# A graph network in one program: bfloat16 matmuls of the preparation that take the tile size of their neighbours in TensorE's order

## The chip, the cores and the metric

The kernel runs on one NeuronCore of a Trainium2 chip. The metric is the device time of one execution in microseconds. The engines are TensorE (PE in the profile; PEld is its loading of weights), VectorE (DVE), ScalarE (ACT), GpSimd (POOL), and SyncE (SP), which issues most DMAs.

## What is computed

128 graphs of 128 nodes with 64 features go through two layers, each with a residual sum and a layer norm over the features:

```python
mask = (adj > 0.0)
diff = x[:, :, None, :] - x[:, None, :, :]
h = relu((x @ W1a)[:, :, None, :] + diff @ W1b + b1)      # 192 wide
x = layernorm(x + einsum('bjkh,bjk->bjh', h, mask) @ W2 + deg * b2)

agg = adj @ x
h = elu(elu(agg @ V1 + c1) @ V2 + c2)                     # 128 wide
x = layernorm(x + h @ V3 + c3)
```

The adjacency is symmetric in its pattern, about 6% dense, and its entries are drawn at random. The first layer is the costly one: for each node j and each of its neighbours k it needs relu(a_j + c_k), where a and c are projections of x.

## The kernel before

Graphs are taken two at a time: 64 pairs, called rounds here. Within a pair, nodes are sorted by their number of neighbours, so that nodes of like degree stand together in nine blocks (`BLOCKS`, line 43). A block has a range of nodes and a number of slots, one for each possible neighbour; its columns are nodes times slots: 162, 66, 168, 112, 168, 154, 169, 154 and 170 for blocks 0 to 8. A neighbour's c_k is fetched into its column by a matmul with a one-hot matrix.

The steps of a pair, with the lines of the kernel before:

- `prepare` (line 523): the mask and the degrees (DVE, L532), keys (POOL), `spread`, which lays the degrees along the rows by matmul (PE, L545 and L547), ranks by comparison (DVE, L554), the permutation matrix `permb` (DVE, L561).
- `sort_x` (with `project_a`): the features sorted (PE, L578), project_a (PE, L592), the copy `aj` (ACT, L599), then a correction for empty slots: two short matmuls (PE, L612 and L615), the product `ea` (DVE, L621), POOL work.
- `sort_mask` (line 631): mask and permutation sorted and transposed (PE, L637 and L640), copied out (ACT, L645 and L647), the prefix sum along neighbours (PE, L651: one matmul of 256 columns), copied (ACT, L654), and nine writes of one-hot blocks into the tile `oh` (DVE, L661). `oh` is one tile of 128 partitions by 2 x 1323 columns: 1323 for the first graph, then 1323 for the second, each with blocks 0 to 8 in order.
- `turn`: transposes of adjacency and features (PE, L676 and L677). `project_c`: c with 64-row tiles (PE, L694), with a bias (PE, L697), split into three bfloat16 parts `cp`.
- `unit` (line 831), nine times: ACT copies a_j into a PSUM bank (L839), the gather adds c (PE, L851: 18 matmuls in two column tiles of 64, one a graph), DVE sums |.| over slots (L860). Four PSUM banks go round.
- `finish` (line 766): hm (POOL), project (PE, L776, L780, L783), unsort (PE, L793), norm, aggregate (PE, L800), hidden1 (PE, L809), hidden2 (PE, L815), last (PE, L820, L822), norm, output.

TensorE's array is used in three tile sizes: full (128 by 128), two column tiles of 64 (the gathers, the sorting of x, the short correction, aggregate), and two row tiles of 64 (L694). Which is used follows from the operands' shapes.

The order of all work is made in Python while the program is built: `Flow` runs each step as a generator that yields its engine, an assumed cost, the events that it needs and the number of PSUM banks. At each turn `run` takes the step that is ready first by these assumed times, and among those ready within `NEAR` of it (`NEAR_PE` on TensorE) the one with the lowest rank: its due time from the table `DUE`, plus `HOLD` where TensorE would change its mode. Steps in column tiles are marked `PE:t`; all others, row tiles too, count as full. Engines then execute in exactly the order that came out. Waits are added from the tiles that are written and read.

Of the kernel before, what the change touches and what calls it, by code (L numbers as in the profile page):

```python
# [87 lines left out]
class Flow:  # L88
# [6 lines left out]

    LAG = 0.2
    NEAR = 0.1
    NEAR_PE = 0.03  # L100
    SWITCH = 0.1
    HOLD = 0

    def __init__(self, banks):
        self.clock = {}
# [48 lines left out]
    def run(self):  # L154
        while self.threads:
            ready = [(t, th) for t, th in ((self._ready(th[4]), th) for th in self.threads)
                     if t is not None]
            t, th = min(ready, key=lambda r: (r[0], r[1][0], r[1][1]))
            first = th[4][0].split()[0].partition(":")[0]
            near = t + (self.NEAR_PE if first == "PE" else self.NEAR)  # L160
            t, th = min((r for r in ready if r[1][4][0].split()[0].partition(":")[0] == first
                         and r[0] <= near), key=lambda r: self._rank(r[1]))
            engine, cost, after, banks, fn = th[4]
            args = []
            if banks:
                self.free.sort(key=lambda f: f[0])
                args = [self.free.pop(0)[1] for _ in range(banks)]
            fn(*args)
            for e in engine.split():
                e, _, mode = e.partition(":")  # L170
                self.clock[e] = t + cost
                if e == "PE":
                    self.mode = mode
            self._next(th, ([t + cost + self.LAG], *args))


def sparse(tc, env):
# [9 lines left out]
    flow = Flow([ps_m.tile([P, 512], F32, name=f"m{i}") for i in range(4)])  # L187
# [1 line left out]
    EV = {}  # L189


    ROUND = 11.14
    AHEAD = 3
    PACE = ROUND / NB

    DUE = {
        "prepare": (-34.32, -34.43, -29.25, -33.33, -26.26),
        "sort_x": (-25.05, -19.47, -20.79, -15.63, -11.78, -14.33, -11.15, -5.27, -5.97),
        "sort_mask": (-24.98, -24.21, -19.11, -17.63, -31.08, -14.67, -12.13, -9.2, -7.19, -6.42,
                      -4.21, -1.99, -12.24, -7.24),  # L200
        "turn": (-25.52, -21.42),
        "project_c": (-19.53, -25.02, -26.5, -19.03, -18.18, -16.73, -23.86),
        "finish": (7.83, 15.84, 19.72, 16.78, 21.09, 22.6, 28.99, 31.57, 29.07, 31.37, 30.6,
                   34.42, 35.7, 33.91, 37.94, 41.34, 41.72, 43.55, 44, 37.02, 51.36),
        "unit": (-1.1, 0.98, 2.36),
    }

    def pace(u):
# [7 lines left out]
    def event(*key):  # L216
        return EV.setdefault(key, [])
# [13 lines left out]

    def pool(n):
        return 0.15 + n * 0.0022

    def flat(t):
        return t.rearrange("p s n -> p (s n)")
# [22 lines left out]
    iotb = const([P, P], BF16, "iotb")  # L259
# [38 lines left out]
    def made(*names):  # L298
        return [event("const", name) for name in names]
# [223 lines left out]
    def prepare(p):  # L523

        a = ADJ[p]
        d = S[p] = {}
        mk = d["mk"] = prep.tile([P, 2, N], BF16, name="mk")
        deg = prep.tile([P, 2], F32, name="deg")

        def count():  # L530
            for s in range(2):
                nc.vector.tensor_scalar(mk[:, s, :], a[:, s, :], 0.0, 0.0, op0=OP.is_gt,  # L532
                                        op1=OP.add, accum_out=deg[:, s:s + 1])
        ev, = yield ("DVE", 0.54, [event("load", p)], 0, count)
# [6 lines left out]
        ev, = yield ("POOL PORT", 0.43, [ev] + made("jcol"), 0, keys)  # L541

        def spread(key):
            for s in range(2):
                nc.tensor.matmul(key[:, s * N:(s + 1) * N], degb[:, s:s + 1].to_broadcast([P, P]),  # L545
                                 identb, start=True, stop=True)
            nc.tensor.matmul(key[:, 2 * N:3 * N], small, iotb, start=True, stop=True)  # L547
        ev, key = yield ("PE", 0.17, [ev] + made("identb", "small", "iotb"), 1, spread)
# [37 lines left out]
    def project_a(p, xsT, ev):  # L586
# [16 lines left out]
        happened(ev, "aj", p)  # L603
        have = ev
        sa = prep.tile([P, 3, N], F32, name="sa", bufs=3)
        evs, = yield ("POOL PORT", 0.95, [have] + made("srow"), 0, lambda: nc.gpsimd.tensor_mul(sa, aj, srow))  # L606

        def short(eb):

# [21 lines left out]
    def sort_mask(p, ev):  # L631
# [2 lines left out]

        def sort(t):
            for s in range(2):
                nc.tensor.matmul(t[:, s * N:(s + 1) * N], d["mk"][:, s, :], permb[:, s, :],  # L637
                                 start=True, stop=True)
# [11 lines left out]
        ev, vps = yield ("PE", 0.11, [evm] + made("prefix"), 1,  # L650
                         lambda vps: nc.tensor.matmul(vps[:, :2 * N], prefix, flat(mtp),  # L651
                                                      start=True, stop=True))
# [17 lines left out]
    def turn(p):  # L670

        d, a, xx = S[p], ADJ[p], XX[p]

        def transpose(t):
            for s in range(2):
                nc.tensor.transpose(t[:, s * N:(s + 1) * N], a[:, s, :], ident)  # L676
            nc.tensor.transpose(t[:, 2 * N:3 * N], flat(xx), ident)  # L677
        ev, t = yield ("PE", 0.4, [event("load", p)] + made("ident"), 1, transpose)
# [37 lines left out]
    def norm(yps, ev, name, rest, shift):  # L716
# [22 lines left out]
        ev, = yield ("POOL PORT", 1.24 if shift else 0.88, [ev] + made("mhalf"), 0, factors)  # L739
        o = work.tile([P, 2, F], F32, name=name, bufs=6)  # L740

        def apply():
# [23 lines left out]
    def finish(p):  # L766
# [40 lines left out]
        def hidden1(zb):  # L807
            for s in range(2):
                nc.tensor.matmul(zb[:, s * N:(s + 1) * N], v1p[:, s, :], agg,  # L809
                                 start=True, stop=True)  # L810
        ev, zb = yield ("PE", 0.45, [ev] + made("v1p"), 1, hidden1)
        h1, ev = yield from elu(zb, ev, "h1", 0)

        def hidden2(zb):
            nc.tensor.matmul(zb[:, :2 * N], v2s, h1, start=True, stop=True)  # L815
        ev, zb = yield ("PE", 0.44, [ev], 1, hidden2)
        h2, ev = yield from elu(zb, ev, "h2", 1)

        def last(t):
# [300 lines left out]
```

## Time and profile before

| what | value |
|---|---|
| median of the runs (three) | 771.95 us |
| range of the runs | 770.51 to 772.46 us |
| the profiled execution's own time | 770.88 us |
| its span | 769.0 us |
| mean granted TensorE clock | 0.994 |
| gather matmuls (L851) | 10368 records, 228 ns each, 110 ns for each load of weights |

A float32 matmul stands as two records of TensorE. The duration of a matmul's record holds the way through the array, so neighbours overlap; how fast TensorE goes is read from the distance between starts. "Idle before" in the groups is counted between records, so it misses a wait that is shorter than this overlap.

### The profile page before, as it was taken

The numbers are of one execution on the slowest core, as the hardware profiler recorded it, in microseconds if no ns is written. First come the engines' busy times: TensorE is split into PE (matmuls) and PEld (weight loads), VectorE is DVE, ScalarE is ACT, GpSimd is POOL, SyncE is SP. The second block draws the span as 40 slices with busy tenths as digits, with TensorE's granted clock in tenths as the row PEclk, the third lists the DMA queues.
The fourth block names the chain that finished last, engine by engine and source line by source line (L and its number), as shares of the span: only waits on it lengthen the run. The fifth ranks groups of instructions, "written<-read, shape, count | busy, mean of one in ns | idle before, by whom it ended". The sixth has DMA issues, their size and how long they took to land.

```text
span 769.0 us, 35363 instructions
## 1 busy us (share of the span) xinstructions
PE 746.9 (97%) x14487; PEld 671.7 (87%) x14488; DVE 717.1 (93%) x2357; ACT 702.0 (91%) x1990; POOL 432.9 (56%) x806
## 2 busy tenths in 40 slices
PE   7899999999999999999999999999999999999993
PEld 5688998999899899889889889989899889989992
DVE  7999999999999999999999999999999999999982
ACT  5788999999999999999999999999999999999974
POOL 6445565665665665655555555556566566566542
PEclk9999999999999999999999999999999999999997
DMA  3011110110111011011011011011011011100000
GB/s 81 3 24 26 27 30 21 27 31 20 27 30 27 21 30 30 16 31 30 18 30 31 17 30 30 21 27 30 21 27 30 21 27 30 27 20 21 10 9 18
DMA packets 63881, 19.75 MB, mean 26 GB/s; under 512 B 46816, under 2 KB 63712, under 8 KB 63712
## 3 DMA queue, kind: packets, MB, share of 16 engines
q1 hardware_dynamic: 63008, 17.12, 9.6%
q8 instruction: 115, 1.88, 1.1%
q14 instruction: 54, 0.44, 0.2%
q10 hardware_dynamic: 704, 0.30, 0.2%
HBM read 13.14 MB, written 4.19 MB: 23 GB/s over the span
## 4 chain that ended last, share of the span: by engine, by line
PE 93%; DVE 3%; ACT 1%; DMA 1%; issue 1%; POOL 0%; ACTq 0%; DVEq 0%
PE e L851 44%; PE m L592 6%; PE m L776 5%; PE m L694 5%; PE m L809 4%; PE m L815 4%; PE m L822 4%; PE m L793 3%; PE m L578 2%; PE m L676 2%; PE m L800 2%; PE m L637 2%; PE m L651 2%; PE m L780 1%; PE m L697 1%; DVE sums L860 1%
## 5 line engine op out<-in xcount | busy, mean ns | idle before, releaser
L851 PE MATMUL e<-oh,cp 128*64 128x162 bf16 (+3 forms) x10368 | 390.6, 228 | 1.8 <-ACT e L839 1.5
L851 PEld LDWEIGHTS <-cp 128*64 128x64 bf16 x10368 | 356.8, 110 | 30.6 <-issue 22.6
L860 DVE TENSOR_REDUCE sums<-e 128x54 f32<-128x486 f32 (+8 forms) x576 | 330.2, 608 | 12.8 <-PE e L851 12.4
L839 ACT COPY e<-aj 128x504 f32<-128x504 f32 (+6 forms) x576 | 309.7, 558 | 7.2 <-DVE sums L860 6.7
L661 DVE TENSOR_TENSOR oh<-vp,slotc 128x336 bf16<-128x336 bf16 (+6 forms) x576 | 167.6, 319 | 1.8 <-PE e L851 1.7
L606 POOL TENSOR_TENSOR sa<-aj,srow 128x384 f32<-128x384 f32 x64 | 65.3, 1020 | 121.6 <-ACT aj L599 118.8
L733 POOL TENSOR_SCALAR ve<-st 128x2 f32<-128x2 f32 x128 | 24.5, 191 | 156.1 <-DVE st L726 150.5
L734 POOL TENSOR_TENSOR rs<-ve,mhalf 128x2 f32<-128x2 f32 x128 | 88.9, 695 | 10.6
L713 POOL TENSOR_TENSOR cp<-r,cp 128x512 bf16<-128x512 f32 x64 | 74.2, 1159 | 13.2 <-ACT cp L711 13.2
L771 POOL TENSOR_TENSOR hm<-sums,corr 128x384 f32<-128x384 f32 x64 | 64.0, 1000 | 11.8 <-DVE sums L860 11.8
L755 ACT ACTIVATE r<-m,cc 128x256 f32<-128x256 f32 x128 | 64.3, 502 | 4.1 <-PE m L809 3.1
L628 POOL TENSOR_TENSOR corr<-ea,sa 128x384 f32<-128x384 f32 x64 | 64.1, 1001 | 0.9 <-DVE ea L621 0.7
L761 DVE SCALAR_TENSOR_TENSOR h<-m,cc,e 128x256 f32<-128x256 f32 x128 | 60.7, 475 | 3.7 <-ACT e L758 3.7
L592 PE MATMUL m<-xsT,wad 128*128 128x128 f32 x384 | 58.3, 288 | 0.8 <-DVE r L708 0.6
L599 ACT ACTIVATE aj<-m,b1c 128x128 f32<-128x128 f32 x192 | 57.0, 375 | 1.0 <-PE m L592 1.0
L744 ACT ACTIVATE x<-y,nb,rs 128x64 f32<-128x64 f32 x128 | 49.4, 434 | 9.3 <-POOL nb L737 9.2
L758 ACT ACTIVATE e<-r 128x256 f32<-128x256 f32 x128 | 57.6, 451 | 0.1
L554 DVE SCALAR_TENSOR_TENSOR cmp<-m,keyc,tie 128x128 bf16<-128x128 f32 x128 | 39.9, 349 | 16.3 <-PE m L547 15.4
L776 PE MATMUL m<-w2d,hm 128*128 128x128 f32 x384 | 53.9, 277 | 0.3 <-POOL hm L771 0.3
L708 DVE TENSOR_TENSOR r<-m,cp 128x256 f32<-128x256 f32 x128 | 52.2, 411 | 0.8 <-ACT cp L704 0.7
L776 PEld LDWEIGHTS m<-w2d,hm 128*128 128x128 f32 x384 | 48.6, 193 | 1.0 <-POOL hm L771 0.5
L592 PEld LDWEIGHTS m<-xsT,wad 128*128 128x128 f32 x384 | 47.7, 191 | 1.8 <-DVE r L708 0.8
(145 smaller groups left out, 1346.8 us busy)
## 6 DMA issues: line engine op xcount, KB each, us to landing
adj<-in_adj_dram SPq DMA_DIRECT2D x64, 128.0 KB, 2.4
xx<-in_x_dram SPq DMA_DIRECT2D x64, 64.0 KB, 2.3
out_dram<-o SPq DMA_DIRECT2D x64, 64.0 KB, 1.7
degs<-ys SPq DMA_DIRECT2D x64, 1.0 KB, 1.7
w1s<-in_L_gnn_W_dram ACTq DMA_DIRECT2D x2, 96.0 KB, 3.1
w2s<-in_L_gnn_W_dram ACTq DMA_DIRECT2D x2, 48.0 KB, 2.8
v2s<-in_L_gnn_W_dram SPq DMA_DIRECT2D x1, 64.0 KB, 3.0
v1d<-in_L_gnn_W_dram SPq DMA_DIRECT2D x2, 32.0 KB, 2.0
```

The source lines that it names most:

```text
L592: nc.tensor.matmul(aps[:, c * N:(c + 1) * N], wad[:, c, :], xsT, start=True, stop=True)
L606: evs, = yield ("POOL PORT", 0.95, [have] + made("srow"), 0, lambda: nc.gpsimd.tensor_mul(sa, aj, srow))
L628: ev, = yield ("POOL PORT", 1.05, [ev, evs], 0, lambda: nc.gpsimd.tensor_sub(corr, ea, sa))
L661: lambda: nc.vector.tensor_tensor(oh[:, :, c].rearrange("p b (s w) -> p b s w", w=w), vp[:, :, p0:p1].rearrange("p b (o w) -> p b o w", o= ...
L713: lambda: nc.gpsimd.tensor_sub(cp[:, 2], r1, cp[:, 1]))
L734: nc.gpsimd.tensor_tensor(rs, ve, mhalf, op=OP.pow)
L755: lambda: nc.scalar.activation(r, z, AF.Relu, bias=c, scale=-1.0))
L771: lambda: nc.gpsimd.tensor_sub(hm, d["sums"], d["corr"]))
L776: nc.tensor.matmul(yb[:, :2 * O], hm[:, c, :], flat(w2d[:, c]), start=(c == 0), stop=False)
L839: lambda: nc.scalar.copy(e.rearrange("p (c s w) -> p c s w", c=3, w=w), d["aj"][:, :, p0:p1].rearrange("p c (o w) -> p c o w", o=1) .to_br ...
L851: nc.tensor.matmul(e[s * HB:(s + 1) * HB, c * n:(c + 1) * n], cp[:, k, s, c * HB:(c + 1) * HB], oh[:, s, base:base + n], start=False, stop ...
L860: nc.vector.tensor_reduce(d["sums"][:, :, p0:p1], e.rearrange("p (c s w) -> p c w s", c=3, w=w), AX.X, OP.add, apply_absolute_value=True)
```

## The change

Three matmul steps of the preparation (spread, the mask's sort, the prefix sum; all bfloat16, with full-size weights) are no longer fixed at full size. A helper looks at the mode that the planner is in: in column mode it issues two matmuls of 64 columns of weights, each for half of the output's partitions; otherwise one full-size matmul as before. The steps are marked `PE:*`: they neither cost a switch nor change the mode. The choice of the next step is widened on TensorE: besides the steps within `NEAR_PE`, those within `STAY` that keep the mode are candidates. `HOLD` goes from 0 to 4.6, and the round length, the due times and several assumed costs are set anew, so the order on every engine is another.

```diff
-    HOLD = 0
+    STAY = 0.3
+    HOLD = 4.6
...
-        return self.SWITCH if engine == "PE" and mode != self.mode else 0.0
+        return self.SWITCH if engine == "PE" and mode not in ("*", self.mode) else 0.0
+
+    def _same(self, th):
+        return th[4][0].split()[0].partition(":")[2] in ("*", self.mode)
...
+            stay = t + self.STAY if first == "PE" else near
             t, th = min((r for r in ready if r[1][4][0].split()[0].partition(":")[0] == first
-                         and r[0] <= near), key=lambda r: self._rank(r[1]))
+                         and (r[0] <= near or r[0] <= stay and self._same(r[1]))),
+                        key=lambda r: self._rank(r[1]))
...
-                if e == "PE":
+                if e == "PE" and mode != "*":
                     self.mode = mode
...
-    ROUND = 11.14
+    ROUND = 11.02
...
+    def stationary(out, lhsT, rhs, **kw):
+
+        if flow.mode == "t":
+            for h in (slice(0, P // 2), slice(P // 2, P)):
+                nc.tensor.matmul(out[h], lhsT(h), rhs, **kw)
+        else:
+            nc.tensor.matmul(out, lhsT(slice(0, P)), rhs, **kw)
...
-                nc.tensor.matmul(t[:, s * N:(s + 1) * N], d["mk"][:, s, :], permb[:, s, :],
-                                 start=True, stop=True)
-            for s in range(2):
-                nc.tensor.matmul(t[:, (2 + s) * N:(3 + s) * N], permb[:, s, :], identb,
-                                 start=True, stop=True)
-        ev, t = yield ("PE", 0.22, [ev], 1, sort)
+                stationary(t[:, s * N:(s + 1) * N], lambda h: d["mk"][:, s, h], permb[:, s, :],
+                           start=True, stop=True)
+            for s in range(2):
+                stationary(t[:, (2 + s) * N:(3 + s) * N], lambda h: permb[:, s, h], identb,
+                           start=True, stop=True)
+        ev, t = yield ("PE:*", 0.22, [ev], 1, sort)
...
-        ev, vps = yield ("PE", 0.11, [evm] + made("prefix"), 1,
-                         lambda vps: nc.tensor.matmul(vps[:, :2 * N], prefix, flat(mtp),
-                                                      start=True, stop=True))
+        ev, vps = yield ("PE:*", 0.12, [evm] + made("prefix"), 1,
+                         lambda vps: stationary(vps[:, :2 * N], lambda h: prefix[:, h], flat(mtp),
+                                                start=True, stop=True))
...
-        ev, t = yield ("PE", 0.45, [ev, event("permT", p)], 1, unsort)
+        ev, t = yield ("PE", 0.4, [ev, event("permT", p)], 1, unsort)
```

Spread is edited in the same way. In the table `DUE` 60 of the 61 due times change, for example those of the mask's sort, whose last nine entries are the one-hot writes:

```diff
-        "sort_mask": (-24.98, -24.21, -19.11, -17.63, -31.08, -14.67, -12.13, -9.2, -7.19, -6.42,
-                      -4.21, -1.99, -12.24, -7.24),
+        "sort_mask": (-22.9, -22.04, -18.56, -16.14, -41.84, -14.24, -11.23, -8.29, -6.76, -7.93,
+                      -22.64, -7.2, -15.34, -6.22),
```

More of the change, by code (lines that the diff above doesn't have):

```diff
@@ L196, in sparse @@
     DUE = {
-        "prepare": (-34.32, -34.43, -29.25, -33.33, -26.26),
-        "sort_x": (-25.05, -19.47, -20.79, -15.63, -11.78, -14.33, -11.15, -5.27, -5.97),
-        "sort_mask": (-24.98, -24.21, -19.11, -17.63, -31.08, -14.67, -12.13, -9.2, -7.19, -6.42,
-                      -4.21, -1.99, -12.24, -7.24),
[L201 to L205, printed above, removed]
+        "prepare": (-37.44, -49.42, -29.4, -33.36, -27.02),
+        "sort_x": (-24.63, -21.69, -22.19, -14.84, -13.99, -17.43, -13.5, -7.33, -8.93),
+        "sort_mask": (-22.9, -22.04, -18.56, -16.14, -41.84, -14.24, -11.23, -8.29, -6.76, -7.93,
+                      -22.64, -7.2, -15.34, -6.22),
+        "turn": (-23.32, -19.48),
+        "project_c": (-19.19, -19.96, -32.95, -22.38, -23.26, -27.96, -32.98),
+        "finish": (11.26, 18.37, 24.15, 16.83, 23.41, 25.7, 26.85, 35.3, 35.97, 29.7, 29.22,
+                   39.11, 38.35, 34.65, 38.54, 39.19, 35.92, 46.87, 48, 36.75, 54.7),
+        "unit": (-1.18, 8.27, 2.36),
     }
@@ L540, in keys @@
             nc.gpsimd.tensor_sub(keyc, deg, jcol)
-        ev, = yield ("POOL PORT", 0.43, [ev] + made("jcol"), 0, keys)
+        ev, = yield ("POOL PORT", 0.32, [ev] + made("jcol"), 0, keys)
         def spread(key):
             for s in range(2):
[L545 to L548, printed above, removed]
+                stationary(key[:, s * N:(s + 1) * N],
+                           lambda h: degb[:, s:s + 1].to_broadcast([P, h.stop - h.start]),
+                           identb, start=True, stop=True)
+            stationary(key[:, 2 * N:3 * N], lambda h: small[:, h], iotb, start=True, stop=True)
+        ev, key = yield ("PE:*", 0.17, [ev] + made("identb", "small", "iotb"), 1, spread)
         pos = prep.tile([P, 2], F32, name="pos")
@@ L605, in project_a @@
         sa = prep.tile([P, 3, N], F32, name="sa", bufs=3)
-        evs, = yield ("POOL PORT", 0.95, [have] + made("srow"), 0, lambda: nc.gpsimd.tensor_mul(sa, aj, srow))
+        evs, = yield ("POOL PORT", 1.0, [have] + made("srow"), 0, lambda: nc.gpsimd.tensor_mul(sa, aj, srow))
         def short(eb):
@@ L677, in transpose @@
             nc.tensor.transpose(t[:, 2 * N:3 * N], flat(xx), ident)
-        ev, t = yield ("PE", 0.4, [event("load", p)] + made("ident"), 1, transpose)
+        ev, t = yield ("PE", 0.33, [event("load", p)] + made("ident"), 1, transpose)
         turned = d["turned"] = prep.tile([P, 3, N], F32, name="turned", bufs=9)
@@ L738, in factors @@
                                             op0=OP.mult, op1=OP.mult)
-        ev, = yield ("POOL PORT", 1.24 if shift else 0.88, [ev] + made("mhalf"), 0, factors)
+        ev, = yield ("POOL PORT", 1.27 if shift else 0.97, [ev] + made("mhalf"), 0, factors)
         o = work.tile([P, 2, F], F32, name=name, bufs=6)
@@ L810, in hidden1 @@
                                  start=True, stop=True)
-        ev, zb = yield ("PE", 0.45, [ev] + made("v1p"), 1, hidden1)
+        ev, zb = yield ("PE", 0.49, [ev] + made("v1p"), 1, hidden1)
         h1, ev = yield from elu(zb, ev, "h1", 0)
@@ L815, in hidden2 @@
             nc.tensor.matmul(zb[:, :2 * N], v2s, h1, start=True, stop=True)
-        ev, zb = yield ("PE", 0.44, [ev], 1, hidden2)
+        ev, zb = yield ("PE", 0.48, [ev], 1, hidden2)
         h2, ev = yield from elu(zb, ev, "h2", 1)
```

## The prediction

> **What bounds the kernel now.** I read the page's busy table first, then the stretches, then the timeline of TensorE (PE) through one round (one pair of graphs), and last VectorE (DVE) around one-hot writes.
>
> ```profile
> span 769.0 us, 35363 instructions
> PE 746.9 (97%) x14487; PEld 671.7 (87%) x14488; DVE 717.1 (93%) x2357; ACT 702.0 (91%) x1990; POOL 432.9 (56%) x806
> ...
> PE 93%; DVE 3%; ACT 1%; DMA 1%; issue 1%; POOL 0%; ACTq 0%; DVEq 0%
> ```
>
> ```profile
> 300.00:400.00 100.00, 100.00 (x1998) 91.32 (x1998) 96.04 (x317) 95.42 (x273) 57.23 (x104) 1.00 0.11 27
> ```
>
> TensorE is the bound and in the middle it never stands idle; but DVE and ACT are at 96% and 95%, so there is little room for a new order to be out of step. The records of matmuls overlap, so I don't add durations: I subtract starts. The timeline of one round:
>
> ```profile
> 312.82 1.46 PE L851 MATMUL e<-oh,cp 128*64 128x169 bf16 x36
> 314.22 0.28 PE L651 MATMUL m<-mtp,prefix 128*128 128x256 bf16 x1
> 314.34 0.83 PE L776 MATMUL m<-w2d,hm 128*128 128x128 f32 x6
> ...
> 316.71 0.66 PE L809 MATMUL m<-agg,v1p 128*128 128x128 f32 x4
> 317.30 0.85 PE L851 MATMUL e<-oh,cp 128*64 128x170 bf16 x18
> ...
> 319.27 1.28 PE L851 MATMUL e<-oh,cp 128*64 128x168 bf16 x36
> 320.48 0.28 PE L637 MATMUL m<-permb,mk 128*128 128x128 bf16 x2
> ...
> 322.18 0.65 PE L815 MATMUL m<-h,v2s 128*128 128x256 f32 x2
> 322.76 0.27 PE L851 MATMUL e<-oh,cp 128*64 128x168 bf16 x2
> ```
>
> The round repeats: a gather (L851) starts after hidden2 (L815) at 311.326 and again at 322.759, 11.433 us later, hardly differing from about 62 to 720 us. It goes into full-size tiles twice (at L651 and L637), back to 64-column tiles twice (after L809 and L815), and inside the second full-size stretch into row tiles and out (L694, L697): six switches.
>
> DVE around the write of the last one-hot block, the one 340 columns wide:
>
> ```profile
> 316.33 0.72 DVE L661 TENSOR_TENSOR oh<-vp,slotc 128x308 bf16<-128x308 bf16 x3
> 316.97 0.29 DVE L721 TENSOR_TENSOR y<-m,xx 128x128 f32<-128x128 f32 x1
> ...
> 318.20 0.69 DVE L860 TENSOR_REDUCE sums<-e 128x51 f32<-128x510 f32 x1 [0.20 <-PE e L851]
> 318.81 0.54 DVE L621 SCALAR_TENSOR_TENSOR ea<-aj,m 128x384 f32<-128x384 f32 x1
> ```
>
> The third of the three writes of the first line (start 316.716, 0.334 long) is done at 317.06, and the next pair's gathers begin at 318.10: 1.04 us of slack. Keep it in mind.
>
> **What the Trainium skill says.** "TensorEngine Tiling (Array Packing)", section Key Properties: changing the tiling mode drains TensorE. The trace agrees: the last matmul of L809 starts at 305.662 and streams 0.111, the gather starts at 305.867, so 94 ns lie empty; of L815, 96 ns. The same page, Restrictions: column tiling gives up fast weight load. Agrees: a 64-column bf16 load takes 110 ns against 97 for a full one. "TensorE: Matmul & The Clock Gate", Back-to-back issue gap: N columns at 2.4 GHz plus 2.5 ns a matmul; gathers of 170 columns come 73 ns apart in each tile, as that gives. The same page's heading table: DVE's queue is strictly first in, first out; the order of its records agrees, and my main case hangs on it.
>
> **The change part by part.** The planner's new constants (due times, HOLD 4.6, STAY, costs) write another order for every engine, which I read from the built program. In a settled round TensorE now does: gathers of blocks 7, 8 (with the short L629/L632, sort of x, aggregate, prefix as two column tiles), blocks 0, 1, 2; full: unsort, hidden1, [row tiles: project_c], spread; gathers of blocks 3 to 6; full: last, hidden2, project_a, project, transposes, mask sort; and again. Six switches again: only the prefix moves into column mode; all told they fall from 406 to 394, the 12 being at the two ends. So the saving that the edit speaks of hardly exists in the middle. Matmuls rise by 92 (63 prefixes split, the rest in the first microseconds).
>
> TensorE's work per round, from gaps between starts in the old trace (ns). Full stretches before: 3082 (L651 to L809) and 2282 (L637 to L815), sum 5364; column-mode stretches 6069; together 11433. After:
> - unsort (L793 in the old numbering) 495, as at 746.29, where it follows a gather and its first weights are not loaded ahead; 394 in the settled round, where they are. Hidden1 (L809) 593 with a switch behind it, as now. Project_c (L694, L697) 635 + 68, as now. Spread (L545, L547) 113 + 149, the latter 56 and 93 for the switch behind it, as at 49.64. Together 2053.
> - last (L820, L822) 67 + 446 and hidden2 (L815) 488: from 740.78 to 741.78 the old trace runs just these, in this order, after a gather. Project_a (L592) 667, what the float32 group behind hidden2 takes there; 751 in the old round, where its first load stands behind matmuls of one column. Project (L776, L780, L783) 655 + 174 + 54. Transposes (L676, L677) 252 + 109, as at 45.55 behind short bfloat16 matmuls. Mask sort (L637, L640) 112 + 205, as at 25.95 with the switch behind it. Together 3229.
> - column mode: gathers 5163 (nine matmuls a tile in each of nine blocks, columns by 2.4 plus 2.5) + 27 of small gaps that stand in the old round, L629/L632 111, sort of x 248, aggregate 218, prefix 109 (two tiles side by side, 256 columns each, unknown: 109 to 220), two exits at 115 (seen: 106 to 139), two entries at 25: 6156.
>
> Sum 11438, against 11433: +5 ns, a draw, with some 40 ns of doubt. What project_a and last gain (-84, -94, hidden2 -93), unsort (+101) and the switches behind spread and mask sort (+93, +83) give back.
>
> **The wait.** Gathers of block 0 wait, in both programs, for the write of block 8 of the same pair's one-hot tile: the second matmul (sequence 1) waits for DVE's count to reach it. Sequence 1's block 0 lies between block 8's columns of sequence 0 and of sequence 1, and the dependence spans the range. Such a wait shows once in the old trace's ramp: the second matmul of the gather at 54.23 goes at 54.309, 43 ns after the one-hot write below gave its signal, and the gather takes 0.83 to the next step where 0.65 is its streaming: 0.07 of the rest is the wait, the remainder the switch behind it.
>
> ```profile
> 53.90 0.35 DVE L661 TENSOR_TENSOR oh<-vp,slotc 128x338 bf16<-128x338 bf16 x1 [0.66 <-PE e L851]
> ```
>
> ```profile
> 54.23 0.90 PE L851 MATMUL e<-oh,cp 128*64 128x168 bf16 x18
> ```
>
> For block 0, slack was 1.04 us. In the new DVE order that write comes behind the reduction of block 7 and `ea`, and that reduction waits for block 7's gather, just after a full stretch. Counting from the start T of block 7's last matmul:
> - DVE: starts the reduction at T+280 (block 8 in the old round: last matmul 317.914, reduction 318.202; 7 less for 154 columns), 546 for it (start to start), 461 for `ea`, 331 for the write, 12 to the signal and 43 until TensorE goes (its usual time from release to start in the early waits): T+1674.
> - TensorE: 67 + 111 + 660 (block 8) + 248 + 218 + 109 + 5 = T+1418.
> So it stands still 256 ns a round; nothing later catches up, for TensorE is the bound. If prefix costs 220 as two tiles, the same round results (the wait shrinks as much). Behind the waiting matmul all of TensorE is queued: blocks 0 to 2, unsort, and ACT and DVE after these. Bounds of the wait: 150 to 330 ns.
>
> Round after: 11438 + 256 = 11694, +261. It is settled from the third hidden2 (52 gathers issued) to that with 556: 56 rounds, +14.6 us. Ends: 12 switches fewer at about 0.12 is -1.4, of which about half falls in time where TensorE waits anyway: -0.7. Profiled execution 770.9 (span 769.0 + 1.9): 770.9 + 13.9 = 784.8; the median of the runs shown, 771.95, is 1.1 higher. I take 785. SP's queue and its loads keep their order; loads come three pairs ahead, so no DMA enters. POOL is at 58%.
>
> **Rivals.**
> - A draw, 0.08: the path from block 7 to block 0 on TensorE takes 1.67 us by itself and the rest doesn't grow, so no wait shows. For: sort of x has varied from 218 to 248. Against: 250 ns are missing, and if the prefix supplies them they are in the sum. 771.5, at most 773.
> - The other side, faster, 0.06: no wait, and the planner's own shorter round (11.14 to 11.02 in its constants, 0.12 a round) is real because loads behind long matmuls hide better than my rows: 64 x 0.12 = 7.7, so 764. It decides from about 1.7 us between the two gathers, with project_a and last gaining twice what I count. Against: these rows stand in the trace, and the planner charges TensorE less than 11.43 in both programs.
> - A second wait, 0.10: block 6's gather waits for ACT's copy into its bank. From L714's end ACT does two copies (263 each), the exp (319) and the copy (620), with 290 to begin: 1755, against 1988 on TensorE, 233 of slack. If ACT is 0.4 later, 0.17 x 56 = 9 more: 794.
> - The forecast, 0.76: 785, own range 777 to 791.
>
> **How the numbers follow.** The bounds of the wait give 56 x (-106 to +74 ns), -6 to +4; the sum's 40 ns give 2.2 either way, the ends 3. Together 777 to 791; I put 776 to 793, reaching a little into the second wait. About 0.3%, 2.3 us, is what a measurement here can tell from no change. Slower holds forecast and second wait, 0.86; the draw is mostly within, 0.07; faster 0.07.
>
> **What would show it.** Right: a settled round near 11.69, switches still six, and a gap of some 0.25 us before the second matmul of the 162-column gather, with DVE's 340-column write ending just before. DVE's idle time before the 42-column reduction grows. Wrong: a round of 11.44 or less with that gather unbroken (my DVE path is too long), or a stall at another gather.

## The result, and the profile after

The changed kernel takes 792.33 us (median of four runs, 790.92 to 793.85) against 771.28 us of the kernel before in the same comparison: 21.0 us more, a ratio of 1.027 with an interval of 1.024 to 1.030. The profiled execution of the changed kernel took 793.66 us, 22.8 more than that of the kernel before.

The page and the stretch from 300 to 400 us of the changed kernel, to be laid beside those of before (columns of the stretch: PE, PEld, DVE, ACT, POOL in us of 100, clock, DMA share, GB/s):

```profile
span 791.9 us, 35378 instructions
PE 765.8 (97%) x14579; PEld 682.6 (86%) x14580; DVE 758.5 (96%) x2357; ACT 691.1 (87%) x1990; POOL 439.1 (55%) x806
...
PE 84%; DVE 12%; ACT 1%; issue 1%; DMA 1%; POOL 0%; ACTq 0%; DVEq 0%
```

```profile
300.00:400.00 100.00, 99.46 (x1944) 89.06 (x1943) 98.98 (x304) 90.55 (x265) 57.37 (x101) 1.00 0.11 25
```

TensorE is still busy for 97% of the span and for over 99% of the middle, so the busy table alone hides the loss: a matmul's record holds its way through the array and covers most of a stall. What moved is the chain. DVE's share in it went from 3% to 12%, and DVE is busy for 99% of the middle where it had been for 96%. TensorE's weight loads fell from 91 to 89 us in the same 100: fewer steps were done.

The chain of waits through one round of the changed kernel, in order of time (start, length, engine, tile, line):

```profile
301.34 0.76 PE e L868 x16
302.10 0.02 issue
302.12 0.64 DVE sums L877
302.76 0.46 DVE ea L638
303.22 0.27 DVE oh L678
303.49 0.04 issue
303.53 1.75 PE e L868 x51
...
313.10 0.76 PE e L868 x16
```

This is the forecast path, link by link: the gather of block 7 ends, DVE reduces it, makes `ea`, writes the 340 columns of block 8, and only then does the rest of block 0's gather go. It returns 11.76 us later (301.34 to 313.10). TensorE's timeline of the same place:

```profile
303.10 0.30 PE L247 MATMUL m<-mtp,prefix 128*64 128x256 bf16 x2
303.24 2.04 PE L868 MATMUL e<-oh,cp 128*64 128x162 bf16 x54
305.21 0.66 PE L810 MATMUL m<-ys,permT 128*128 128x64 f32 x4
```

The record 303.24 is block 0's gather, run together with blocks 1 and 2. Its first matmul starts at 303.236 and its second 296 ns later, where 28 ns is usual; from its first matmul to block 1's first are 884 ns, where 18 matmuls in two tiles need 630. The wait costs 254 ns a round. DVE at that place:

```profile
302.12 0.64 DVE L877 TENSOR_REDUCE sums<-e 128x42 f32<-128x462 f32 x1
302.68 0.55 DVE L638 SCALAR_TENSOR_TENSOR ea<-aj,m 128x384 f32<-128x384 f32 x1
303.14 1.30 DVE L678 TENSOR_TENSOR oh<-vp,slotc 128x340 bf16<-128x340 bf16 x2
304.36 0.67 DVE L877 TENSOR_REDUCE sums<-e 128x51 f32<-128x510 f32 x1
```

The third line holds two writes, of 340 and of 132 columns, and takes 1.30 us, where the two should take about 0.6. The groups of DVE, one line of the changed kernel and then one of the kernel before, show which is slow (the last numbers: us in all, mean ns, idle time before):

```profile
L678 DVE TENSOR_TENSOR oh<-vp,slotc 128x132 bf16<-128x132 bf16 x64 | 61.2, 956 | 0.0
```

```profile
L661 DVE TENSOR_TENSOR oh<-vp,slotc 128x132 bf16<-128x132 bf16 x64 | 15.6, 244 | 0.0
```

The write of the 132 columns takes 956 ns instead of 244, each time. GpSimd's timeline of the changed kernel has an instruction beside it, the subtraction `corr`, which is released by the same `ea`:

```profile
303.30 1.03 POOL L645 TENSOR_TENSOR corr<-ea,sa 128x384 f32<-128x384 f32 x1 [0.39 <-DVE ea L638]
```

In the order of before, `corr` stood elsewhere (309.88) and the write was not held. This was not in the forecast.

Where the 22.9 us between the two spans are: 0.7 before the first gather (starts at 22.76 and 23.41), 20.2 from there to the last matmul of the last gather, 2.0 after it (22.9 to the end of the span before, 24.9 after). In the settled part a round is 11.767 us against 11.433, and 57 times 0.334 is 19.0 of the 20.2. Three rounds of the changed kernel, near 200, 389 and 577 us, are longer by another 0.18 us each; the trace doesn't show why.

The 2.0 at the end go with TensorE's clock, and not with the new order. The pages give it in 40 slices of the span, in tenths of full speed: first the kernel before, then the changed kernel, then e5 of the experiments below, which has the changed order too.

```profile
PEclk9999999999999999999999999999999999999997
PEclk9999999999999999999999999999999999999995
PEclk9999999999999999999999999999999999999997
```

In these three the clock is at half for the last 9.1, 17.5 and 8.5 us, and from the first matmul of the last block's gather to the end of the span are 23.5, 25.5 and 23.1 us. The other profiles of this document fall into the same two groups, 23.2 to 23.7 us and 25.1 to 25.6, and each group holds kernels of both orders. What decides when the clock falls is not shown.

### The profile page after: what moved, and what is told of

It is laid out like the page before. It is cut to its first block, busy times and chain, and to the rows that moved or that the text cites. A ratio compares the mean times of both kernels' runs of the same rounds, so it can differ in the third digit from the quotient of the medians.

```text
span 791.9 us, 35378 instructions
## 1 busy us (share of the span) xinstructions
PE 765.8 (97%) x14579; PEld 682.6 (86%) x14580; DVE 758.5 (96%) x2357; ACT 691.1 (87%) x1990; POOL 439.1 (55%) x806
## 4 chain that ended last, share of the span: by engine, by line
PE 84%; DVE 12%; ACT 1%; issue 1%; DMA 1%; POOL 0%; ACTq 0%; DVEq 0%
PE e L868 41%; PE m L793 5%; PE m L609 5%; DVE sums L877 5%; PE m L711 5%; PE m L810 5%; PE m L826 4%; PE m L832 4%; PE m L839 4%; DVE ea L638 3%; PE m L249 3%; DVE oh L678 2%; PE m L693 2%; PE m L797 1%; PE m L714 1%; PE m L837 1%
## 5 line engine op out<-in xcount | busy, mean ns | idle before, releaser
L868 PE MATMUL e<-oh,cp 128*64 128x162 bf16 (+3 forms) x10368 | 394.9, 229 | 5.3 <-ACT e L856 1.9
L868 PEld LDWEIGHTS <-cp 128*64 128x64 bf16 x10368 | 348.1, 110 | 32.1 <-issue 19.5
L877 DVE TENSOR_REDUCE sums<-e 128x54 f32<-128x486 f32 (+8 forms) x576 | 342.8, 606 | 7.5 <-PE e L868 2.5
L678 DVE TENSOR_TENSOR oh<-vp,slotc 128x308 bf16<-128x308 bf16 (+6 forms) x576 | 214.5, 402 | 1.4 <-PE e L868 1.2
L645 POOL TENSOR_TENSOR corr<-ea,sa 128x384 f32<-128x384 f32 x64 | 65.7, 1026 | 22.4 <-DVE ea L638 22.4
L772 ACT ACTIVATE r<-m,cc 128x256 f32<-128x256 f32 x128 | 60.3, 471 | 5.4 <-PE m L826 3.5
L609 PEld LDWEIGHTS m<-xsT,wad 128*128 128x128 f32 x384 | 52.4, 191 | 3.1
L775 ACT ACTIVATE e<-r 128x256 f32<-128x256 f32 x128 | 54.6, 427 | 0.2
L609 PE MATMUL m<-xsT,wad 128*128 128x128 f32 x384 | 53.4, 276 | 0.0
L725 DVE TENSOR_TENSOR r<-m,cp 128x256 f32<-128x256 f32 x128 | 48.1, 417 | 0.8 <-ACT cp L721 0.8
L711 PE MATMUL m<-wc,turned 64*128 64x256 f32 x256 | 45.1, 428 | 1.1 <-ACT slots L499 1.0
```

What stands on the lines that cost most here:

```text
L609: nc.tensor.matmul(aps[:, c * N:(c + 1) * N], wad[:, c, :], xsT, start=True, stop=True)
L645: ev, = yield ("POOL PORT", 1.05, [ev, evs], 0, lambda: nc.gpsimd.tensor_sub(corr, ea, sa))
L678: lambda: nc.vector.tensor_tensor(oh[:, :, c].rearrange("p b (s w) -> p b s w", w=w), vp[:, :, p0:p1].rearrange("p b (o w) -> p b o w", o= ...
L711: nc.tensor.matmul(cps[s][:, :cols], d["turned"][k, 2, :], wc[k, :], start=True, stop=False)
L868: nc.tensor.matmul(e[s * HB:(s + 1) * HB, c * n:(c + 1) * n], cp[:, k, s, c * HB:(c + 1) * HB], oh[:, s, base:base + n], start=False, stop ...
L877: nc.vector.tensor_reduce(d["sums"][:, :, p0:p1], e.rearrange("p (c s w) -> p c w s", c=3, w=w), AX.X, OP.add, apply_absolute_value=True)
```

## The experiments

Eleven kernels. A "round" is the distance between the starts of the same matmul in two rounds following each other, near 300 us. The ratio is to the kernel before in the same comparison, whose medians were 772.21, 771.95 and 771.36 us in the three sets.

| kernel | median us | ratio and interval | round us |
|---|---|---|---|
| changed, one-hot tile by blocks (e1) | 786.47 | 1.017 (1.013 to 1.022) | 11.68 |
| before, one-hot tile by blocks (e2) | 766.41 | 0.992 (0.989 to 0.995) | 11.373 |
| changed, `ea` later (e3) | 775.49 | 1.004 (1.003 to 1.006) | 11.459 |
| changed, all at full size (e4) | 792.68 | 1.027 (1.022 to 1.031) | 11.766 |
| changed, `corr` in thirds (e5) | 791.34 | 1.026 (1.024 to 1.029) | 11.766 |
| changed, by blocks and thirds (e6) | 769.64 | 0.998 (0.997 to 0.999) | 11.410 |
| before, even starts (e7) | 769.36 | 0.997 (0.996 to 0.998) | 11.373 |
| before, the edit alone (e8) | 776.63 | 1.006 (1.004 to 1.008) | 11.522 |
| before, even starts and by blocks (e9) | 766.94 | 0.994 (0.993 to 0.996) | 11.370 |
| changed, even, by blocks, `ea` later (e10) | 771.41 | 1.000 (0.998 to 1.001) | 11.408 |
| changed, even starts (e11) | 788.17 | 1.021 (1.019 to 1.023) | 11.685 |

### The wait alone, the collision alone, both

First the wait is taken away, and nothing else: the one-hot tile is laid out block by block, both graphs of a block side by side, so that block 0's columns no longer lie between those of block 8.

```diff
-        oh = d["oh"] = prep.tile([P, 2, E], BF16, name="oh", bufs=5)
+        oh = d["oh"] = prep.tile([P, 2 * E], BF16, name="oh", bufs=5)
...
-                             oh[:, :, c].rearrange("p b (s w) -> p b s w", w=w),
+                             oh[:, 2 * base:2 * (base + n)]
+                             .rearrange("p (b s w) -> p b s w", b=2, w=w),
...
-                                         oh[:, s, base:base + n],
+                                         oh[:, 2 * base + s * n:2 * base + (s + 1) * n],
```

> The changed kernel with the one-hot tile laid out block by block (each block's columns for both graphs together), so that the gather of block 0 no longer waits for the write of block 8; the order of every engine is the same. Wait alone: 0.256 us a round over 57 rounds is gone, 792.3 becomes about 778, and DVE's 132-column write stays slow. DVE nearly bound, because that write stands 0.8 us behind a GpSimd operation: DVE idles only 0.09 us a round now, so at most 0.09 x 57 = 5 us come back, about 787, with DVE never idle. Order alone (TensorE's work and switches cost all): 792 unchanged.

Measured: 786.47 us. Block 0's gather takes its 630 ns again, but only 5.9 us of the 21 come back. The stretch of this kernel shows what is next in line:

```profile
300.00:400.00 100.00, 99.49 (x1961) 89.68 (x1956) 99.95 (x311) 90.93 (x265) 57.99 (x105) 1.00 0.12 27
```

DVE is busy for 99.95%, with the held write still at 955 ns. Its chain of waits runs over DVE and ACT into another gather, that of block 5 (816 ns instead of 600):

```profile
313.10 0.48 DVE mk L548 x4
313.58 0.59 DVE sums L878
314.19 1.09 ACT e L857 x2
315.29 0.40 ACT r L773
315.69 0.54 ACT cp L722 x2
316.23 0.32 ACT e L776
316.54 0.49 ACT e L857
317.08 0.86 PE e L869 x18
```

A reduction that comes late frees its bank late, ACT copies into it late, and the gather waits. So a second limit, at 11.68 us a round, stood right behind the wait's 11.77.

Next the opposite: the wait stays, and the collision is made shorter. `corr` becomes three instructions of 128 columns.

```diff
-        ev, = yield ("POOL PORT", 1.05, [ev, evs], 0, lambda: nc.gpsimd.tensor_sub(corr, ea, sa))
+        def correct():
+            for c in range(3):
+                nc.gpsimd.tensor_sub(corr[:, c, :], ea[:, c, :], sa[:, c, :])
+        ev, = yield ("POOL PORT", 1.05, [ev, evs], 0, correct)
```

> The changed kernel with GpSimd's subtraction corr (one instruction of 128x384 elements, 1.03 us) made as three instructions of 128x128, so that a one-hot write of VectorE that begins beside it can be held for a third of the time only. The wait at the second matmul of block 0's gather is untouched. If that wait alone sets the round (the chain through the reduction, ea and the 340-column write starts when TensorE ends the gather before, whatever VectorE does later): the 132-column write falls from 956 ns to 400 to 650, VectorE from 99% to 95 or 97%, and the round stays at 11.77, the time at 789 to 794. If VectorE's load sets the round and the wait only shows it: the round falls by what the write gives back, 0.3 to 0.5 us, and the time goes to 765 to 775. GpSimd's work grows by two starts of an instruction, some 0.2 us a round, with room for it at 55% busy.

Measured: 791.34 us and a round of 11.766. The write falls from 956 to 467 ns (GpSimd's third takes 461), and DVE from 99% to 96%:

```profile
300.00:400.00 100.00, 99.46 (x1944) 89.06 (x1943) 95.84 (x305) 92.22 (x267) 60.03 (x120) 1.00 0.11 24
```

TensorE's and the loads' numbers are to the digit those of the changed kernel. Half a microsecond of DVE's time in every round is worth nothing while the wait is there: the chain starts when TensorE ends block 7, whatever DVE does later. The wait sets the round.

Both edits together, the two diffs above in one kernel:

> Both causes taken away in the changed kernel's own order: the one-hot tile laid out block by block (no wait of block 0's gather for block 8's write) and corr in three instructions. If two limits lie one behind the other, the wait and then VectorE with the held write: neither of the edits alone brings more than 6 us, both together bring the round to TensorE's own work, 11.767 less the wait's 0.254 less 0.03 to 0.06 for the layout, about 11.46 to 11.48, and the time to 773 to 777. If the layout had already brought all there is and what is left is the order's own work on TensorE: 785 to 787, as with the layout alone. If three subtractions hold VectorE as long as one did: 785 to 787 with the 132-column write still at about 950.

Measured: 769.64 us, 22.7 less than the changed kernel, where one edit brought 5.9 and the other about 1. That is more than the 773 to 777 expected; a second effect of the layout, shown further below, had been put too low. TensorE fills the stretch:

```profile
300.00:400.00 100.00, 100.00 (x1982) 91.56 (x1978) 98.29 (x315) 94.04 (x274) 61.46 (x122) 1.00 0.11 25
```

The two limits lay one behind the other, and that is shown from both sides. With both gone, the changed order is 0.25% faster than the kernel before (though not faster than that kernel with the same layout).

A third way to the same place moves one instruction: `ea` is issued just ahead of `corr`, and so falls behind the two one-hot writes and one reduction in DVE's queue.

```diff
-        ev, = yield ("DVE", dve(3 * N), [ev], 0,
-                     lambda: nc.vector.scalar_tensor_tensor(
+        def ends():
+            nc.vector.scalar_tensor_tensor(
...
+        ev, = yield ("DVE", dve(3 * N), [ev], 0, lambda: held.append(ends))
...
+        def correct():
+            while held:
+                held.pop(0)()
+            nc.gpsimd.tensor_sub(corr, ea, sa)
```

> The changed kernel with the product ea taken out from between the reduction of block 7 and the one-hot write of block 8 and put behind the next reduction; layout and waits as changed. DVE's way to that write is 0.46 us shorter, so the wait of 0.26 us is gone, and GpSimd's correction starts later, so the 132-column write should be fast again (0.25 instead of 0.96 us). Wait alone: 778, same as with the new layout. DVE nearly bound: 778 here against 787 with the layout alone. Order alone: 792.

Measured: 775.49 us, 17 of the 21 us back by the place of one instruction of 0.55 us. It undoes both limits at once: the 340-column write is no longer behind `ea`, and the 132-column write is over (238 ns) when `corr` begins.

### Is it the column tiles, or the order?

In the changed kernel's own order, all three steps are made at full size again:

```diff
-        if flow.mode == "t":
+        if False:
```

> The changed kernel in the same order, but every one of the three steps at full size: switches rise from 393 to 526, two a round around the prefix sum, which lies between the gathers of blocks 7 and 0. Wait: the 0.2 us a round that the switches cost fall into the time that TensorE waits anyway, so 792 to 795. Order alone (no wait that counts): 0.2 x 57 = 12 us more, 804.

Measured: 792.68 us and a round of 11.766, as with column tiles, although the program has 133 tile switches more. The switches that are added lie ahead of the waiting gather, and TensorE only waits the less: block 0's gather starts 2.17 us after that of block 7 and not 1.97, but its second matmul comes after 2.27 us in both kernels. While the wait stands, the saved switches are worth nothing. Without it the column tiles might be worth some 0.2 us a round in this order, an estimate from these starts; no run has the changed order at full size without the wait.

The reverse: the edit in the order of the kernel before. The three steps take the mode of the step ahead of them and nothing is moved.

```diff
-                nc.tensor.matmul(key[:, s * N:(s + 1) * N], degb[:, s:s + 1].to_broadcast([P, P]),
-                                 identb, start=True, stop=True)
+                stationary(key[:, s * N:(s + 1) * N],
+                           lambda h: degb[:, s:s + 1].to_broadcast([P, h.stop - h.start]),
+                           identb, start=True, stop=True)
...
-        ev, vps = yield ("PE", 0.11, [evm] + made("prefix"), 1,
-                         lambda vps: nc.tensor.matmul(vps[:, :2 * N], prefix, flat(mtp),
-                                                      start=True, stop=True))
+        ev, vps = yield ("PE", 0.11, [evm] + made("prefix"), 1,
+                         lambda vps: stationary(vps[:, :2 * N], lambda h: prefix[:, h], flat(mtp),
+                                                start=True, stop=True))
```

> The edit alone, in the order of the kernel before: the three steps take the tile mode that TensorE is in when they come, and nothing is moved. The prefix step and the mask sort follow a gather and become column tiles, the spread stays at full size; the number of tile switches is 401 against 405, since the switch only moves behind the step. If the loss of the change lies in the new order and not in the edit: the round grows by the exits only, 0 to 0.04 us, and the time is 771 to 774. If column tiles of these steps cost what the change lost: 785 or more. If they save as such: 768 or less.

Measured: 776.63 us, above what the order theory allowed by 2.6 and far below the other. The round grew by 0.09 us, and one place holds all of it. TensorE's timeline there, of the kernel before and then of this one:

```profile
301.39 1.46 PE L851 MATMUL e<-oh,cp 128*64 128x169 bf16 x36
302.78 0.28 PE L651 MATMUL m<-mtp,prefix 128*128 128x256 bf16 x1
...
303.57 0.34 PE L780 MATMUL m<-cp,mtp 128*128 128x64 bf16 x6
```

```profile
302.22 1.46 PE L860 MATMUL e<-oh,cp 128*64 128x169 bf16 x36
303.51 0.28 PE L239 MATMUL m<-mtp,prefix 128*64 128x256 bf16 x2
303.72 0.94 PE L785 MATMUL m<-w2d,hm 128*128 128x128 f32 x6
304.49 0.34 PE L789 MATMUL m<-cp,mtp 128*128 128x64 bf16 x6
```

From the gathers to L780, now L789, are 2.18 us before and 2.27 with the edit. An exit from column mode is counted here from the first matmul of the last block to the first one in the new mode, less what the block's nine matmuls in a tile stream (600 ns for 154 columns). With a full-size prefix the exit costs 132 ns in front of it, and the float32 weights of the project step are loaded while it streams (the load starts at 302.786, the prefix at 302.784): its matmuls follow at 111 ns. With a prefix in column mode that load starts only at 303.719, the exit stands in front of the project step itself (106 ns), and then the second matmul of that comes after 213 ns instead of 111; another 30 ns, the lag of one column tile that the next part explains, stand ahead of the prefix. The mask's sort, followed by a bfloat16 step, costs the same either way (847 and 846 ns with the gather ahead and the first matmul behind). So a short full-size bfloat16 step at an exit is no waste: it covers a load.

### Why the layout made the kernel before faster

The layout on the kernel before, with the diff of e1, was the control of the first experiment.

> The kernel before with the same layout, as a control. All theories: the wait it drops had 1.04 us to spare, so 771 within 0.3%. If the layout itself changed the speed of the one-hot writes or of the gathers, it would show here as more than 2 us.

Measured: 766.41 us, a ratio of 0.992; no theory had it. The starts of the matmuls show a drift. In a gather, matmuls of the two column tiles alternate, and in the kernel before the second tile's starts fall behind by about 3 ns with every matmul of block 5's gather: 6, 9, 12, 16 up to 29 ns (at 300.574); in most other blocks by less. In block 7 it is the first tile that loses. With the layout the offset stays at 3 to 8 ns. The tile of before has 1323 columns a graph, an odd number: the second graph's columns start on an odd element in blocks 0 to 6, the first graph's in blocks 7 and 8, which is how the drift turns round. The rival is the wait that the layout removes. One column of padding tells them apart:

```diff
-        E += n
+        E += n + n % 2
```

> The kernel before with one column of padding behind the block of 169 columns, so that the one-hot tile has an even number of columns and every block begins at an even column in both halves; the tile stays one, and the wait of block 0's gather for block 8's write stays. It asks why the layout alone made the kernel before faster by 0.8%. If the start on an odd bfloat16 element slows one of the two column tiles by 2 to 3 ns a matmul (the offset of the two tiles drifts by that much from matmul to matmul in the trace of before, in the gathers whose second half begins odd, and not with the layout): the drift goes, the exits from column mode fall from 132 and 115 to about 105 and 100, the round to 11.37 to 11.39, and the time to 765 to 768. If it was the wait that the layout took away: the drift may go or stay, and the time is 770 to 772.5.

Measured: a round of 11.373, as with the layout, and 769.36 us, above the expected 768. The drift is gone, and the two exits fall from 132 and 115 to 99 and 100 ns. The timeline of TensorE at the first:

```profile
311.24 1.43 PE L851 MATMUL e<-oh,cp 128*64 128x169 bf16 x36
312.60 0.28 PE L651 MATMUL m<-mtp,prefix 128*128 128x256 bf16 x1
```

1.36 us from gather to prefix, where the line 301.39 above gave 1.39. The exit waits for the tile that is behind: the prefix starts 162 ns after the last gather matmul in both kernels, but that matmul starts 570 ns after its block's first one before and 537 with the padding. That the place of the columns makes the drift is shown, and that it costs the 0.060 us a round as good as shown: one column of padding takes both away, and the two exits hold 48 of the 60 ns. That it is the odd start as such is very likely. The drift turns round where the parity does, and block 6, whose second half still starts odd with the layout, loses half a nanosecond a matmul there as it did before, and nothing once it starts even (e9, next). Why block 6 loses so little and block 5 six times as much stays open.

Padding and layout together on the kernel before (the diff of e1 with the two halves of a block `n + n % 2` columns apart):

> The kernel before with both: every half block of the one-hot tile begins at an even column, and the tile is laid out block by block, so that block 0's gather waits for its own write alone. If the even start is all that the layout brought: as with the padding alone, a round of 11.37 and 0.995 to 0.998 of before. If the removed wait brings something of its own: lower than the padding alone by 0.3% or more, 0.990 to 0.994, with gaps between matmuls that are gone at block 0's gather.

Measured: a round of 11.370 and 766.94 us, a ratio of 0.994. The removed wait changes nothing in the settled round, but it brings something before the rounds have settled: project_c of the eighth pair starts at 79.46 us, and at 80.78 with the padding alone. These 1.3 us are more than half of the 2.4 between the two medians; the rest stays open. The layout alone (0.992) and both edits do not differ clear of their intervals.

The padding alone on the changed kernel (the diff of e7):

> The changed kernel with the padded column alone; wait and held write stay. The drift between the column tiles makes the exits from column mode 139 to 146 ns there, against 122 and 108 in the changed order without it. If the drift is a cost of its own beside the wait: the round falls by 0.04 to 0.07, from 11.767 to 11.70 to 11.73, and the time to 788 to 790. If it falls into the time that TensorE waits anyway, as the tile switches did: 791 to 793.

Measured: a round of 11.685 and 788.17 us. The prefix in column mode falls from 133 to 109 ns, the exit behind block 6 from 146 to 104; block 0's gather still takes 882 to 885 ns. The drift costs the changed kernel 0.082 us a round, 0.02 more than the kernel before and a little more than expected.

And the changed kernel with padding, layout and the later `ea` (the diffs of e9 and e3):

> The changed kernel with every loss found taken away: even starts, one-hot tile block by block, and ea issued just ahead of corr, so that the 132-column write doesn't begin beside it. It asks what the change's order and column tiles are worth on TensorE when nothing waits. If the order is no better on TensorE than that of before (11.41 of the changed order without waits and drift against 11.37): a round of 11.39 to 11.42 and 768 to 770, above the kernel before with the same two edits of the tile. If the placing does bring something once it is freed: a round under 11.35, 765 or less.

Measured: a round of 11.408 and 771.41 us. With all that was found taken away, TensorE's work in the changed order is 0.038 us longer than in the order of before (11.408 against 11.370). The round is also 0.025 us shorter than that of the kernel before, 1.4 us in 57 rounds, and yet the time is the same (771.36 there). Three rounds take 11.76 to 11.78 us, which gives back 1.1 us for a reason that the trace doesn't show, and in the profile the clock is at half for the last 16.1 us, where it was 9.1 before.

## Why the prediction was right, and which of its terms were off

The forecast was 785 us with a range of 776 to 793; the time is 792.33, at the upper edge. It lies above the 777 to 791 that the prediction gave its own case, and inside the range only by the room left for a second wait, which did not occur: so much is luck. The mechanism was the right one; the size was short by 7 us.

- **The wait.** Put at the second matmul of the 162-column gather and at 256 ns; it is there, at 254. That the two agree so closely is partly luck: on TensorE's way there the sort of x was put 30 ns too long and the prefix 24 too short. Its path (the reduction, `ea`, the 340-column write) is the chain of the profile. That it sets the round is shown by e5, where DVE is relieved and nothing moves, and by e4, where TensorE gets more to do and nothing moves.
- **TensorE's work per round: +5 ns forecast, +80 measured** (0.334 less the wait's 0.254). This is the term that was mis-sized. Exits were put at 115 ns each and measured some 150 and 146; the prefix at 109 and measured 133; project at 655 and measured 670, while the sort of x came at 218 instead of 248. The prediction had given the exits a range of 106 to 139 from the old trace without asking what makes them vary. It is the drift of the two column tiles: e11 takes it away, and 82 ns go with it, of which the kernel before had 60 already. The prefix had been called unknown with bounds of 109 and 220, with the remark that a longer prefix shortens the wait. Its 24 ns did not do that: block 0's gather takes 884 ns behind a prefix of 133 and 882 to 885 behind one of 109. The traces show why. The tile that is behind also ends block 7 later, and with it DVE's path starts later: block 7's last matmul comes 578 ns after its first with the drift and 561 without (e11), DVE's reduction after 854 and 834, the waiting matmul of block 0 after 2265 and 2242. Of the 80 ns some 20 are more drift than before, 38 the order's own work (e10 against e9), and some 20 are left for small gaps beside the wait.
- **The draw of switches.** Six a round before and after, so that the saving hardly exists in the middle (405 and 393 in all, by the traces): right, and e4 shows that even 133 more of them are not seen.
- **The ends: -0.7 us forecast, +2.7 in the profiled pair** (0.7 before the first gather, 2.0 after the last). No cost of the order is shown in it. The 2.0 go with the clock at the end, and the first gather starts anywhere from 22.2 to 24.3 us in the kernels with the order of before. In e5, which has the changed order and a clock that falls as late as in the kernel before, the two ends together are 0.3 us shorter than in that kernel, and the whole span is 20.6 us longer. The prediction had no term for the clock at the end.
- **What was missed: the held write.** The prediction left GpSimd with the sentence "POOL is at 58%" and did not ask which instruction stands beside a one-hot write. The Trainium skill, "SBUF — State Buffer", section "SBUF: two separate sides", says that VectorE and GpSimd share a pair of ports which one of them holds for a whole instruction while the other waits, and that a VectorE operation with two inputs in SBUF takes part in this against a GpSimd operation that reads SBUF. The runs agree: 956 ns beside a `corr` of 1026, 467 beside thirds of 461, 235 to 244 beside none. In the time after it costs nothing by itself (e5), as the wait covers it. It decided the repair: e1 left it in place and brought 5.9 us, where e3 and e6, which take both away, brought 17 and 23.
- **The rivals.** The draw and the faster time fell with the first look at block 0's gather. The second wait over ACT's copy does not occur in the changed kernel; it came in e1, at block 5's gather and not block 6's, once the first was gone.

Short by 7: 57 rounds of 0.073 us are 4.2, and in the profiled pair the ends come to about 3.4, most of it the clock.

## What to carry to other kernels

Before a loss is put down to what was edited, take the new order with the old instructions and the old order with the new ones: here the column tiles were worth nothing in the new order while its wait stood and cost 0.6% in the old, and most of the loss came from the place of one instruction, `ea`, on DVE. When the loss is added up, set the clock at the end of the two profiles side by side, before the end of the span is put down to the order. When one wait is removed and little comes back, look at once for the engine that has become full, and at the instruction on it whose mean duration changed, for two limits can stand within 1% of each other. And a dependence on a whole range of a tile is also a matter of layout: columns that are used together should lie together, and it is worth a try to let them begin at an even element.

## What the runs showed of the hardware

- A bfloat16 one-hot write of 132 columns on DVE took 244 ns alone and 956 ns beside a GpSimd subtraction of 1.03 us.
- Two column tiles of TensorE drifted apart by up to 3 ns a matmul, to 29 ns within a gather of 18 matmuls, where the moving columns of one graph start on an odd bfloat16 element and those of the other on an even one; it is paid for the most part at the exit from column mode (132 against 99 ns). One column of padding brought 0.3% of the whole time.
- Leaving column mode straight into a float32 step cost 106 ns and another 102 at its second matmul; with one full-size bfloat16 matmul of 256 columns between, 132 and 11.
- TensorE's clock fell to half for the last 8.5 to 9.5 us of some executions and the last 15.8 to 17.9 us of others, and the stretch from the last block's gather to the end took 23.1 to 23.7 us in the former and 25.1 to 25.6 in the latter, whatever the order of work.
- The kernel before with its one-hot tile laid out by blocks, at 766.4 us (0.992, interval 0.989 to 0.995), is faster than both kernels.
